# Two graph layers on one core: the prologue's vectors, transposes, weight loads and the order of the second pair's steps are rearranged

## The chip, the cores and the metric

The kernel runs on one core of one Trainium2 chip. A core has a matrix engine (TensorE, PE), three engines for elementwise work (VectorE or DVE, ScalarE or ACT, GpSimd or POOL), a queue engine (SyncE, SP) and 16 DMA engines. The metric is the device time of one execution in microseconds (us); the number of a kernel is the median of its runs.

## The reference

Inputs are x, 128 graphs of 128 nodes with 512 features, and adj, 128 matrices of 128 × 128 zeros and ones. All is fp32. Cut to what matters:

```python
# layer 0: graph attention, 8 heads of 64 units, then residual and layernorm
feats = einsum('bnf,hfu->bhnu', x, W)
e     = leaky_relu(e_self[..., :, None] + e_neigh[..., None, :], 0.2)
att   = softmax(e - 1e10 * (1 - adj))
x     = layernorm(x + relu(att @ feats + b0))
# layer 1: hypergraph convolution, twice, then residual and layernorm
H  = adj != 0;  w = adj[:, 0, :]
Dn = 1 / (H @ w);  Be = 1 / H.sum(axis=1)
conv(x, W, b) = Dn * (H @ (Be * (H.T @ (x @ W.T)))) + b
h  = layer_norm(relu(conv(x, W1, b1)), gamma, beta)      # 512 -> 1024
x  = layernorm(x + conv(h, W2, b2) + x)                   # 1024 -> 512
```

(The last line shows both residuals: the one inside the layer and the one around it.)

## The kernel before

The work is cut into 64 pairs of graphs; nodes lie in the 128 partitions. A pair passes through a software pipeline of some four periods of planned length T = 38.6. Its steps, in the names of the code:

- **Nodes and edges.** load (a: the two adjacency matrices; w: their first rows, to all partitions), load_edges (ab: adj in blocks of 32, in packets of 128 bytes), nodes (L334: D as a row, on DVE, seven instructions), write_nodes and spread_nodes (D through DRAM to all partitions, dnb), edges (L388: adj transposed in blocks of 32 by DVE from ab; H and its sums, be), scale_edges (hB = hT·be, L407), propagator (L411: pd = hB·hT on PE), r_evict (R = pd·dnb).
- **Features and attention.** x is transposed by DVE from blocks, for pairs 0 and 1 by PE (x_transpose_first, x_transpose_out). Features (pf) come from W0 with the attention vectors as two more columns. spread_rows and neighbours bring e_neigh through DRAM (rows, rd, nb) to all partitions. masked (L563, POOL) adds the mask, leaky (L579, ACT; for pair 0's last quarter two DVE instructions, L572 and L575), largest (L585, DVE), exponential (L593, ACT). The result is transposed (eT) by DVE from DRAM, for pair 0 by PE (e_transpose_first, pet). attend (pav) multiplies with the features, attended divides, add_bias (POOL), residual and moments, rstds (rsa, POOL), first_shift (sh), first_output.
- **Layer 1.** propagate (pz, L740), z_evict, z_sums; the products of W1 (ph, L775), h_sum, relu, squares; the products of W2 (py, L460); y_sum (L857), y_scale, the second propagation (pq), output. skip (L728) makes o = 2y + b2.

pf, ph and py are chains of seven block products (Strassen-Winograd): each has its own number in brackets here, as pyX(1) or pfW(3), and its products accumulate in banks X, Y and W of PSUM. Copies of X by ACT (L325) and sums by DVE join them. The weights need sums of their blocks for that: prepare_first_sums (W0), prepare_hidden (L228, W1: four sums s1 to s4), prepare_output_block_sums (L286, W2: four sums, by second_sums, L207).

**Weights and vectors.** W1 and W2 come in four blocks each by load_weights, all on ACT's queue. gamma, beta and b1 come by load_vectors (L170) with the partition as the fastest index, so each element is a packet of its own. gamma enters W2: prepare_output multiplies gamma and beta with W2 (pv, L257), prepare_output_sums copies (sums, ACT), prepare_output_spread (gw, bw, L269) spreads the two rows to 128 partitions by PE, prepare_output_blocks (L276) computes W2·gamma − gw in sixteen DVE instructions of 128 × 256.

**What sets the order.** No scheduler does. Every step has a lag and a time; all are put in one list, todo, and sorted by time, and instructions are issued in that order with each engine taking its own in sequence. For the first pairs a table, first, replaces the times by others, so the prologue's order is written out by hand. An engine that waits holds everything behind it in its own queue. A DMA that waits for its data or for a free buffer holds the queue of the engine that issues it.

The lists of the last 40 lines of the code (todo, first, and the loop that follows) are what the change edits most. As an example, this is how the weights' part of it stands:

```python
        (12.1, load_weights, (nc.scalar, w2_blocks, w2t, DH // 2, QU)),
        (13.45, load_vectors, (0,)), (14.05, load_weights, (nc.scalar, w1_blocks, w1t, F // 2, HALF)),
        (15.2, load, (1,)), (15.46, load_edges, (1,)), (16.1, load_vectors, (1,)),
        (79.1, prepare_hidden, (nc.gpsimd, 0)), (79.2, prepare_hidden, (nc.gpsimd, 1)),
```

Of the kernel before, what the change touches and what calls it, by code (L numbers as in the profile page):

```python
# [8 lines left out]
F32 = mybir.dt.float32  # L9
AF = mybir.ActivationFunctionType  # L10
ALU = mybir.AluOpType
# [9 lines left out]
def kernel(  # L21
# [73 lines left out]
    def load(p):  # L95
        s = st[p]
        gs = slice(2 * p, 2 * p + 2)
        s["a"] = work.tile([P, 2, N], F32, tag="a", name=f"a_{p}", bufs=2)
        nc.sync.dma_start(s["a"], adj[gs].rearrange("g n e -> n g e"))
        s["w"] = work.tile([P, 2, N], F32, tag="w", name=f"w_{p}")  # L100
        for g in range(2):
            nc.sync.dma_start(s["w"][:, g, :], adj[2 * p + g, 0, :].partition_broadcast(P))

# [54 lines left out]
    b1_sb = const.tile([P, KH], F32, name="b1_sb")  # L158
    gb = const.tile([P, 2, KH], F32, name="gb")
# [8 lines left out]
    load_edges(0)  # L168

    def load_vectors(some):  # L170
        queue = nc.sync
        if some == 0:
            for t, ap in ((gb[:, 0, :], gamma), (gb[:, 1, :], beta)):
                queue.dma_start(t, ap.rearrange("(k p) -> p k", p=P))
            everywhere(b0_bc, b0, queue)
        else:
            queue.dma_start(b1_sb, b1.rearrange("(k p) -> p k", p=P))
            everywhere(b2_bc, b2, queue)
# [204 lines left out]
    def x_transpose_out(p, s):  # L383
        s["xT"] = work.tile([P, 2, KF, N], F32, tag="xT", name=f"xT_{p}")
        for g in range(2):
            nc.scalar.copy(s["xT"][:, g].rearrange("p k n -> p (k n)"), s["px"][g])

    @step(1, 3.4)  # L388
    def edges(p, s):

        deg = small.tile([P, 2], F32, tag="deg", name=f"deg_{p}")
        hT = work.tile([P, 2, N], F32, tag="hT", name=f"hT_{p}")
        nc.vector.transpose(hT.rearrange("p g (b n) -> p (g b) n", b=NB), s["ab"])
        for g in range(2):
            nc.vector.tensor_scalar(
                hT[:, g, :], hT[:, g, :], 0.0, None, op0=ALU.not_equal, op1=ALU.add,
                accum_out=deg[:, g:g + 1],
            )
# [104 lines left out]
    def plain_features_out(p, s):  # L503
        s["ft"] = fts[p]
        for j in range(2):
            for g in range(2):
                (nc.scalar.copy, nc.vector.tensor_copy)[g](
                    s["ft"][:, g, j * HH:(j + 1) * HH, :UW], by_head(s["pf"][g][j])
                )
# [494 lines left out]
    for t, fn, *args in (  # L1004
# [47 lines left out]
        ("nodes", 2): 130.0, ("write_nodes", 2): 130.1, ("nodes", 3): 150.0,  # L1052
        ("write_nodes", 3): 150.1, ("skip", 0): 128.5,
# [5 lines left out]
    for p, time, fn, *args in (  # L1059
        (0, 11.4, x_transpose_first), (0, 11.5, x_transpose_out),  # L1060
        (0, 12.5, plain_features, 0), (1, 12.55, x_transpose_first),
        (0, 12.6, plain_features, 1), (0, 13.0, plain_features_out),
        (1, 13.8, x_transpose_out), (1, 14.5, plain_features, 0), (1, 14.6, plain_features, 1),
        (1, 15.6, plain_features_out),
# [77 lines left out]
```

## Time and profile before

| what | value |
|---|---|
| median of three runs | 2559.63 us (2559.15 to 2562.24) |
| profiled execution: its time | 2559.59 us |
| its span (first to last instruction) | 2557.8 us |
| instructions | 48296 |
| PE busy from 0 to 120 us | 93.8 us, the sum of the twelve rows of the table by stretch |
| PE busy from 120 to 159 us | 39.0 us |
| granted TensorE clock, whole run | 0.992 |

The profile is of one execution. "Busy" is the time in which an engine runs instructions; the granted clock is the share of its full clock that TensorE got, on average over a stretch. A line of a table by stretch has the stretch in us, its length, then for each of PE, the weight loads of PE (PEld), DVE, ACT and POOL the busy time and in brackets the number of instructions, then the clock, the share of the DMA engines that was busy, and GB/s. A line of waits has the engine, the line that waited, what released it, then the sum of the waiting time in us, the number and the longest. A line of a group has the line of the code, the engine, the operation, out<-in, the shapes, the number, then the busy time in us and the mean in ns, and behind the bar the idle time before it. An answer on one line of the code has the shortest, median and longest duration in ns, then the first and the last start in us.

### The profile page before, as it was taken

Reading aid. Unit: us, or ns where it says so; the run is one execution under the profiler, and the core shown is the slowest. Engines: PE = TensorE matmul, PEld = TensorE weight load, DVE = VectorE, ACT = ScalarE, POOL = GpSimd, SP = SyncE. Lnnn points to the kernel's source line nnn. Section 1 sums busy time; section 2 is a strip of 40 time slices with the busy share of each in tenths; the row PEclk is TensorE's granted clock in tenths of the full one; section 3 lists DMA queues with packets and bytes.
Section 4 is the critical chain, followed back from the end, with each engine's and each line's share of the span. In section 5 each row is a group of like instructions: output and inputs, shape, how many; then the busy total and the mean of one; then the engine's idle time right before and its main releaser. Section 6 shows DMA issues by size and latency. Waiting matters only on the chain.

```text
span 2557.8 us, 48296 instructions
## 1 busy us (share of the span) xinstructions
PE 2519.4 (98%) x16344; PEld 2281.6 (89%) x16344; DVE 2128.8 (83%) x4648; ACT 1514.0 (59%) x4291; POOL 1724.4 (67%) x1805
## 2 busy tenths in 40 slices
PE   7899999999999999999999999999999999999998
PEld 5799999999989999999999899989989998998997
DVE  5888888888888888888888888888888888888875
ACT  3556556557556566566565565565565665665653
POOL 4676766766766776766766666667667667666664
PEclk8999999999999999999999999999999999999999
DMA  6344454444444444444444544444444444444431
GB/s 180 100 141 137 131 145 133 134 143 133 133 140 140 136 137 138 142 133 141 141 134 128 148 138 128 145 130 134 143 139 135 134 141 142 133 127 147 138 111 50
DMA packets 426086, 343.99 MB, mean 134 GB/s; under 512 B 146544, under 2 KB 375408, under 8 KB 425840
## 3 DMA queue, kind: packets, MB, share of 16 engines
q1 hardware_dynamic: 421824, 335.40, 44.5%
q10 hardware_dynamic: 4016, 5.51, 0.7%
q8 instruction: 130, 2.13, 0.3%
q14 instruction: 116, 0.95, 0.1%
HBM read 239.09 MB, written 101.71 MB: 133 GB/s over the span
## 4 chain that ended last, share of the span: by engine, by line
PE 91%; DMA 4%; DVE 2%; issue 1%; POOL 1%; ACT 1%; SPq 0%; ACTq 0%; POOLq 0%; DVEq 0%
PE phX L775 18%; PE pyX L460 14%; PE pfX L460 9%; PE phW L775 9%; PE pav L649 8%; PE pyW L460 8%; PE pz L740 5%; PE phY L775 4%; PE pfW L460 4%; PE pq L898 4%; PE pyY L460 4%; PE pfY L460 2%; DMA nb<-rd 1%; PE pd L416 1%; DMA dnb<-dd_d 1%
## 5 line engine op out<-in xcount | busy, mean ns | idle before, releaser
L563 POOL TENSOR_TENSOR nb<-nb,neg 128x512 f32<-128x512 f32 x256 | 322.1, 1280 | 111.5 <-DMA nb<-rd 63.1
L775 PEld LDWEIGHTS phX<-zS,w_sb 128*128 128x128 f32 x3072 | 363.2, 192 | 32.5 <-issue 31.4
L325 ACT COPY py<-pyX 128x257 f32<-128x257 f32 x189 | 70.6, 374 | 539.3 <-PE pyX L460 535.7
L775 PE MATMUL phX<-zS,w_sb 128*128 128x128 f32 x3072 | 374.5, 276 | 1.8 <-POOL xS L442 1.0
L826 POOL TENSOR_TENSOR sq<-sq 128x512 f32<-128x512 f32 (+2 forms) x384 | 342.5, 892 | 24.0 <-ACT sq L815 2.2
L579 ACT ACTIVATE nb<-nb,ft 128x128 f32<-128x128 f32 x1020 | 323.7, 389 | 19.3 <-POOL nb L563 18.2
L593 ACT ACTIVATE nb<-nb,nm 128x128 f32<-128x128 f32 x1024 | 320.2, 392 | 3.9 <-DVE nm L585 3.8
L696 POOL TENSOR_TENSOR rso<-veo,mhalf 128x2 f32<-128x2 f32 x63 | 44.1, 700 | 333.4 <-DVE veo L694 317.8
L649 PEld LDWEIGHTS pav<-ft,eT 128*128 128x128 f32 x2048 | 253.4, 195 | 7.7
L680 DVE SCALAR_TENSOR_TENSOR y<-y,x 128x512 f32<-128x512 f32 x128 | 153.6, 1200 | 125.1 <-POOL y L673 125.1
L805 ACT ACTIVATE h<-h,b_sb 128x128 f32<-128x128 f32 x768 | 241.0, 392 | 17.1 <-DVE h L790 17.1
L649 PE MATMUL pav<-ft,eT 128*128 128x65 f32 x2048 | 247.3, 275 | 0.0
L460 PE MATMUL pyW<-w_sb,hS 128*128 128x256 f32 x1008 | 240.2, 380 | 6.5 <-DVE y L857 5.4
L460 PE MATMUL pyX<-w_sb,hS 128*128 128x257 f32 x1008 | 242.7, 383 | 0.6 <-ACT py L325 0.6
L460 PE MATMUL pyX<-w_sb,h 128*128 128x257 f32 x1008 | 240.0, 380 | 0.0
L460 PEld LDWEIGHTS pyW<-w_sb,hS 128*128 128x128 f32 x1008 | 189.6, 190 | 39.1 <-DVE y L857 11.5
L673 POOL TENSOR_TENSOR y<-y,b_bc 128x512 f32<-128x512 f32 x128 | 162.5, 1270 | 75.6 <-DVE y L664 75.6
L460 PEld LDWEIGHTS pyX<-w_sb,h 128*128 128x128 f32 x1008 | 187.4, 191 | 24.6
L460 PEld LDWEIGHTS pyX<-w_sb,hS 128*128 128x128 f32 x1008 | 186.5, 190 | 24.8 <-POOL y L673 0.9
L585 DVE TENSOR_REDUCE nm<-nb 128x4 f32<-128x512 f32 x256 | 173.6, 679 | 1.9 <-POOL zS L763 1.3
L442 POOL TENSOR_TENSOR xS<-xT 128x256 f32<-128x256 f32 x124 | 117.7, 949 | 80.6 <-DVE xT L366 80.6
L325 ACT COPY ph<-phX 128x512 f32<-128x512 f32 x192 | 112.3, 585 | 94.5 <-PE phX L775 91.3
(159 smaller groups left out, 5872.5 us busy)
## 6 DMA issues: line engine op xcount, KB each, us to landing
nb<-rd SPq DMA_DIRECT2D x127, 512.0 KB, 6.5
ed<-nb SPq DMA_DIRECT2D x126, 512.0 KB, 3.2
eb<-ed SPq DMA_DIRECT2D x504, 128.0 KB, 2.9
x<-in_x_dram SPq DMA_DIRECT2D x64, 512.0 KB, 7.3
out_dram<-o SPq DMA_DIRECT2D x63, 512.0 KB, 2.9
xb<-in_x_dram SPq DMA_DIRECT2D x248, 128.0 KB, 2.9
a<-in_adj_dram SPq DMA_DIRECT2D x64, 128.0 KB, 6.3
w<-in_adj_dram SPq DMA_DIRECT2D x128, 64.0 KB, 3.9
```

Of the source, the lines that this page charges most:

```text
L325: nc.scalar.copy(t[:, :n], s[kind, "X"][:, :n])
L460: nc.tensor.matmul(to[:, :n], lhs[:, k, :], rhs[:, k, :n], start=bool(start) and k == 0, stop=(k == nk - 1), skip_group_check=True,)
L563: nc.gpsimd.tensor_tensor(t, t, neg[:, :, None, :].to_broadcast([P, NB, HH, B]), op=ALU.add)
L579: nc.scalar.activation(t, t, AF.Prelu, bias=s["ft"][:, g, h, 0:1], alpha=SLOPE)
L585: nc.vector.tensor_reduce(s["nm"][:, g, hs], scores(p, s, g, hs).rearrange("p b h j -> p h b j"), AX.XY, ALU.max, negate=True,)
L593: nc.scalar.activation(t, t, AF.Exp, bias=s["nm"][:, g, h:h + 1])
L649: nc.tensor.matmul(t[:, h * (U + 1):(h + 1) * (U + 1)], s["eT"][:, g, q * HH + h, :], s["ft"][:, g, q * HH + h, 2:], start=True, stop=True,)
L673: nc.gpsimd.tensor_tensor(s["y"][:, g, :], s["y"][:, g, :], b0_bc, op=ALU.add)
L680: nc.vector.scalar_tensor_tensor(y, y, 0.0, s["x"][:, g, :], op0=ALU.max, op1=ALU.add)
L775: nc.tensor.matmul(to[:, m * N:(m + 1) * N], w[:, k, m * P:(m + 1) * P], rhs[:, k, :], start=bool(start) and m == 0 and k == 0, stop=(k == ...
L805: nc.scalar.activation(dst[:, k, :], src[:, k, :], AF.Relu, bias=b1_sb[:, c:c + 1])
L826: nc.gpsimd.tensor_tensor(t[:, :n, :], t[:, :n, :], t[:, n:2 * n, :], op=ALU.add)
```

## The change

It touches the prologue alone, which is the time before pairs follow each other in the steady order.

- gamma, beta and b1 are loaded as rows, 8 × 128 each, into one tile of 24 partitions (vec_rows); one PE transpose and one ACT copy make the columns (vecs). The loads stand early on SP's queue.
- adj of pairs 0 and 1 is transposed by PE (adj_transpose_first, bank pt) instead of by DVE from ab; the ab loads of these two pairs go.
- W1's blocks: the first two are issued by ACT, the other two by SP, the last first.
- Both copies of pair 1's features per half are on DVE.
- Three of the four hidden sums are on POOL (2, 0, 1, in this order), one on DVE; before it was two and two.
- The copies of sums are on DVE, not on ACT; gw and bw come ahead of attend(0,0,0) on PE; the first eight of the sixteen blocks of W2·gamma come between the two graphs' attended(0), the other eight in two groups of four.
- nodes(1) on DVE goes from before pair 0's scores to behind them, ahead of the first copies of eT. edges(1) goes behind sh of pair 0, pd_1 behind pz_0 on PE, R_1 behind h's first sum.
- skip(0) goes behind the h sums of pair 0, the two W2 sums on DVE are split and go further back, nodes(2) goes behind the first part of attended(1) of pair 1, ahead of the last feature sum (and of rows_2). The load of adj for pair 2 goes from 16.3 to 79.5, for pair 3 from 131 to 141.

The diff, cut to its core:

```diff
-    def load(p):
+    def load_adj(p):
         s = st[p]
-        gs = slice(2 * p, 2 * p + 2)
         s["a"] = work.tile([P, 2, N], F32, tag="a", name=f"a_{p}", bufs=2)
-        nc.sync.dma_start(s["a"], adj[gs].rearrange("g n e -> n g e"))
+        nc.sync.dma_start(s["a"], adj[2 * p:2 * p + 2].rearrange("g n e -> n g e"))
+    def load_first_row(p):
...
-    load_edges(0)
-    def load_vectors(some):
...
+    vec_rows = work.tile([3 * KH, P], F32, tag="neg", name="vec_rows", bufs=2)
+    for i, ap in enumerate((gamma, beta, b1)):
+        nc.sync.dma_start(vec_rows[i * KH:(i + 1) * KH], ap.rearrange("(k p) -> k p", p=P))
+    everywhere(b0_bc, b0, nc.sync)
+    load_adj(1)
...
+    def prepare_vectors():
+        t = bank("vecs_T")
+        nc.tensor.transpose(t[:, :3 * KH], vec_rows, ident[:3 * KH, :3 * KH])
+        nc.scalar.copy(vecs.rearrange("p v k -> p (v k)"), t[:, :3 * KH])
...
-            nc.scalar.copy(made["sums"][:, j * QU:(j + 1) * QU], made["pv"][j][:2, :QU])
+            nc.vector.tensor_copy(made["sums"][:, j * QU:(j + 1) * QU], made["pv"][j][:2, :QU])
...
+    def adj_transpose_first(p, s):
+        s["pt"] = bank(f"pt_{p}")
         for g in range(2):
+            nc.tensor.transpose(s["pt"][:, g * N:(g + 1) * N], s["a"][:, g, :], ident)
...
-        nc.vector.transpose(hT.rearrange("p g (b n) -> p (g b) n", b=NB), s["ab"])
+        if p < 2:
+            src = s["pt"][:, :2 * N].rearrange("p (g n) -> p g n", g=2)
+        else:
+            src = hT
+            nc.vector.transpose(hT.rearrange("p g (b n) -> p (g b) n", b=NB), s["ab"])
...
-                (nc.scalar.copy, nc.vector.tensor_copy)[g](
+                (nc.vector.tensor_copy if g or p else nc.scalar.copy)(
...
-        (13.45, load_vectors, (0,)), (14.05, load_weights, (nc.scalar, w1_blocks, w1t, F // 2, HALF)),
-        (15.2, load, (1,)), (15.46, load_edges, (1,)), (16.1, load_vectors, (1,)),
-        (79.1, prepare_hidden, (nc.gpsimd, 0)), (79.2, prepare_hidden, (nc.gpsimd, 1)),
+        (13.05, prepare_vectors, ()),
+        (14.05, load_weights, (nc.scalar, w1_blocks[:2], w1t, F // 2, HALF)),
+        (15.2, load_first_row, (1,)),
+        (15.46, load_weights, (nc.sync, w1_blocks[:1:-1], w1t, F // 2, HALF)),
+        (16.1, everywhere, (b2_bc, b2, nc.sync)),
+        (79.0, prepare_hidden, (nc.gpsimd, 2)), (79.1, prepare_hidden, (nc.gpsimd, 0)),
+        (79.2, prepare_hidden, (nc.gpsimd, 1)), (110.6, prepare_hidden, (nc.vector, 3)),
...
-        (79.0, prepare_rows, ()), (79.4, prepare_output_sums, ()),
-        (98.0, prepare_output_spread, ()), (98.1, prepare_output_bias, ()),
-        (110.6, prepare_hidden, (nc.vector, 2)), (110.7, prepare_hidden, (nc.vector, 3)),
-        (117.8, prepare_output_blocks, (slice(0, 1),)),
-        (118.1, prepare_output_blocks, (slice(1, 2),)),
-        (123.3, prepare_output_blocks, (slice(2, 4),)),
+        (78.3, prepare_rows, ()), (78.86, prepare_output_sums, ()),
+        (78.92, prepare_output_spread, ()), (79.35, prepare_output_bias, ()),
+        (99.75, prepare_output_blocks, (slice(0, 2),)),
+        (117.8, prepare_output_blocks, (slice(2, 3),)),
+        (118.1, prepare_output_blocks, (slice(3, 4),)),
         (126.5, prepare_output_block_sums, (nc.gpsimd, slice(0, 2))),
-        (132.0, prepare_output_block_sums, (nc.vector, slice(2, 4))),
+        (134.5, prepare_output_block_sums, (nc.vector, slice(2, 3))),
+        (137.5, prepare_output_block_sums, (nc.vector, slice(3, 4))),
...
-        ("r_evict", 0): 99.65,
-        ("spread_rows", 1): 15.72, ("nodes", 1): 15.8, ("write_nodes", 1): 15.85,
-        ("edges", 1): 15.9, ("scale_edges", 1): 15.95, ("neighbours", 1): 80.1,
-        ("propagator", 1): 98.2, ("spread_nodes", 1): 80.3, ("r_evict", 1): 110.9,
-        ("leaky", 0, 1, 1): 77.0,
+        ("r_evict", 0): 99.76,
+        ("spread_rows", 1): 15.72, ("nodes", 1): 78.67, ("write_nodes", 1): 78.68,
+        ("edges", 1): 110.4, ("scale_edges", 1): 110.5, ("neighbours", 1): 80.1,
+        ("propagator", 1): 117.76, ("spread_nodes", 1): 80.3, ("r_evict", 1): 121.8,
+        ("leaky", 0, 1, 1): 77.65,
...
-        ("attended", 0): 99.7,
+        ("attended", 0, 0): 99.7, ("attended", 0, 1): 99.8,
...
-        ("nodes", 2): 130.0, ("write_nodes", 2): 130.1, ("nodes", 3): 150.0,
-        ("write_nodes", 3): 150.1, ("skip", 0): 128.5,
+        ("nodes", 2): 139.5, ("write_nodes", 2): 139.6, ("nodes", 3): 150.0,
+        ("write_nodes", 3): 150.1, ("skip", 0): 132.5,
...
-            todo.append(({2: 16.3, 3: 131.0}.get(p, p * T), load, (p,)))
+            todo.append(({2: 79.5, 3: 141.0}.get(p, p * T), load, (p,)))
```

More of the change, by code (lines that the diff above doesn't have):

```diff
@@ L93 @@
     st = [{} for _ in range(PAIRS)]
-    def load(p):
+    def load_adj(p):
         s = st[p]
-        gs = slice(2 * p, 2 * p + 2)
         s["a"] = work.tile([P, 2, N], F32, tag="a", name=f"a_{p}", bufs=2)
-        nc.sync.dma_start(s["a"], adj[gs].rearrange("g n e -> n g e"))
+        nc.sync.dma_start(s["a"], adj[2 * p:2 * p + 2].rearrange("g n e -> n g e"))
+    def load_first_row(p):
+        s = st[p]
         s["w"] = work.tile([P, 2, N], F32, tag="w", name=f"w_{p}")
@@ L102, in load @@
             nc.sync.dma_start(s["w"][:, g, :], adj[2 * p + g, 0, :].partition_broadcast(P))
+    def load(p):
+        load_adj(p)
+        load_first_row(p)
     def load_rows(p, s):
@@ L156 @@
     )
-    b1_sb = const.tile([P, KH], F32, name="b1_sb")
-    gb = const.tile([P, 2, KH], F32, name="gb")
+    vecs = const.tile([P, 3, KH], F32, name="vecs")
+    gb, b1_sb = vecs[:, :2], vecs[:, 2]
     everywhere(an_bc, a_neigh, nc.scalar)
@@ L167 @@
     load(0)
-    load_edges(0)
-    def load_vectors(some):
[L171 to L178, printed above, removed]
+    vec_rows = work.tile([3 * KH, P], F32, tag="neg", name="vec_rows", bufs=2)
[3 more added lines that the diff above has]
+    load_adj(1)
     w2_sb = const.tile([P, 7, KH // 2, QU + 1], F32, name="w2_sb")
@@ L381, in x_transpose_first, with x_transpose_out @@
                 )
-    def x_transpose_out(p, s):
-        s["xT"] = work.tile([P, 2, KF, N], F32, tag="xT", name=f"xT_{p}")
+    def x_transpose_out(p, s, g):
+        if g == 0:
+            s["xT"] = work.tile([P, 2, KF, N], F32, tag="xT", name=f"xT_{p}")
+        nc.scalar.copy(s["xT"][:, g].rearrange("p k n -> p (k n)"), s["px"][g])
+    def adj_transpose_first(p, s):
+        s["pt"] = bank(f"pt_{p}")
         for g in range(2):
-            nc.scalar.copy(s["xT"][:, g].rearrange("p k n -> p (k n)"), s["px"][g])
+            nc.tensor.transpose(s["pt"][:, g * N:(g + 1) * N], s["a"][:, g, :], ident)
     @step(1, 3.4)
@@ L392, in edges @@
         hT = work.tile([P, 2, N], F32, tag="hT", name=f"hT_{p}")
-        nc.vector.transpose(hT.rearrange("p g (b n) -> p (g b) n", b=NB), s["ab"])
+        if p < 2:
[3 more added lines that the diff above has]
+            nc.vector.transpose(hT.rearrange("p g (b n) -> p (g b) n", b=NB), s["ab"])
         for g in range(2):
             nc.vector.tensor_scalar(
-                hT[:, g, :], hT[:, g, :], 0.0, None, op0=ALU.not_equal, op1=ALU.add,
+                hT[:, g, :], src[:, g, :], 0.0, None, op0=ALU.not_equal, op1=ALU.add,
                 accum_out=deg[:, g:g + 1],
@@ L1059 @@
     for p, time, fn, *args in (
-        (0, 11.4, x_transpose_first), (0, 11.5, x_transpose_out),
+        (0, 11.4, x_transpose_first), (0, 11.5, x_transpose_out, 0), (0, 11.5, x_transpose_out, 1),
         (0, 12.5, plain_features, 0), (1, 12.55, x_transpose_first),
-        (0, 12.6, plain_features, 1), (0, 13.0, plain_features_out),
-        (1, 13.8, x_transpose_out), (1, 14.5, plain_features, 0), (1, 14.6, plain_features, 1),
-        (1, 15.6, plain_features_out),
+        (0, 12.6, plain_features, 1), (0, 12.65, adj_transpose_first),
+        (0, 13.0, plain_features_out), (1, 13.1, x_transpose_out, 0), (1, 13.8, x_transpose_out, 1),
+        (1, 14.5, plain_features, 0), (1, 14.6, plain_features, 1),
+        (1, 15.6, plain_features_out), (1, 97.9, adj_transpose_first),
         (0, 78.8, e_transpose_first, 0, 0), (0, 78.85, e_transpose_first, 0, 1),
```

## The prediction

> **What bounds the kernel now.** I read the page's busy shares and chain of work first, then a table of busy time by stretch, then the waits of TensorE (PE) and ScalarE (ACT), then groups and single instructions of VectorE (DVE) and GpSimd (POOL) in the prologue. The page says that nothing but TensorE can be late for most of the run:
>
> ```profile
> PE 2519.4 (98%) x16344; PEld 2281.6 (89%) x16344; DVE 2128.8 (83%) x4648; ACT 1514.0 (59%) x4291; POOL 1724.4 (67%) x1805
> PE 91%; DMA 4%; DVE 2%; issue 1%; POOL 1%; ACT 1%; SPq 0%; ACTq 0%; POOLq 0%; DVEq 0%
> ```
>
> The table by stretch (length, busy PE, weight loads, DVE, ACT, POOL, then granted clock) shows where the other 38 us lie:
>
> ```profile
> 40.00:50.00 10.00, 7.19 (x30) 5.80 (x31) 8.20 (x15) 4.90 (x16) 2.91 (x5) 0.61 0.74 112
> 50.00:60.00 10.00, 8.92 (x28) 5.96 (x26) 5.82 (x14) 1.69 (x4) 4.50 (x4) 0.50 0.57 131
> 60.00:70.00 10.00, 8.07 (x50) 7.91 (x51) 8.69 (x15) 7.01 (x19) 9.29 (x9) 0.70 0.01 2
> 70.00:80.00 10.00, 7.88 (x66) 7.37 (x66) 9.90 (x24) 7.99 (x26) 6.04 (x6) 1.00 0.46 157
> 80.00:90.00 10.00, 5.63 (x32) 4.45 (x31) 9.84 (x16) 4.98 (x17) 4.81 (x5) 1.00 0.31 76
> 90.00:100.00 10.00, 9.83 (x31) 8.44 (x32) 3.40 (x10) 1.84 (x5) 8.32 (x8) 0.50 0.23 60
> 120.00:159.00 39.00, 39.00 (x256) 35.20 (x255) 32.24 (x72) 23.56 (x68) 26.90 (x29) 1.00 0.45 136
> ```
>
> From 120 us on PE never idles (39.00 of 39.00). So the change can only move the moment at which that steady train starts. I take as its mark pz_1, the propagate product of pair 1, at 115.71 us; everything behind it is shifted rigidly. Before the mark there are idle PE and half clock: 42.1 to 66.0 us and 89.9 to 100.15 us at 0.5. Three waits carry it:
>
> ```profile
> PE pfX L460 <- ACT pf L325: 4.5, 1, 4.5
> PE pyW L460 <- DVE y L857: 1.3, 1, 1.3
> ACT ft L507 <- DMA w<-in_adj_dram: 12.5, 1, 12.5
> ```
>
> The first: PE stands from 85.66 to 90.17 because a copy by ACT stands behind relu of h(1,0), which stands behind DVE, which does skip(0), nodes(2) and two weight sums first (79.65 to 87.86). The half clock after it covers 10.24 us of work that would need 5.1. The third: ACT hangs at the issue of the last two W1 loads until 34.4.
>
> **What the Trainium skill says.** "SBUF — State Buffer", section "SBUF: two separate sides": DVE and POOL share a port pair as a lock held for a whole instruction; a DVE operation with two SBUF inputs blocks against POOL. The trace agrees. Beside POOL's two sums (the last line, here from a view of that line) one of the two L407 took 2111 ns, the other 281, and L572 1658 against the 692 of L575, which has the same shape and ran free:
>
> ```profile
> L407 DVE TENSOR_SCALAR hB<-hT,deg 128x128 f32<-128x128 f32 x2 | 2.3, 1194 | 0.0
> L572 DVE TENSOR_TENSOR nb<-nb,ft 128x512 f32<-128x512 f32 x1 | 1.7, 1658 | 0.0
> L575 DVE SCALAR_TENSOR_TENSOR nb<-nb 128x512 f32<-128x512 f32 x1 | 0.7, 692 | 0.0
> L234 POOL TENSOR_TENSOR w_sb<-w_sb x1: 2417/2417/2417, 40.5 to 40.5; 128x1024 f32<-128x1024 f32 x1
> ```
>
> "TensorE: Matmul & The Clock Gate", Part 1: after idle time of about one window of 3.4 us PE gets half its clock. The trace agrees: 0.5 after the idle stretches 37.94–41.79 and 85.66–90.17. Part 4 adds that transposes don't count as busy in the same way, which fits the half clock that stays through 46–59. "DMA: Bandwidth & Descriptors", section "Issuing engines are not separate DMA queues": a second queue saves issue time only. That fits the third wait above, which is issue time.
>
> **The change, part by part.**
>
> *Vectors as rows.* Three loads of 1024 elements, two of which landed at 16.2 and 19.3, become three short ones and a transpose. First use is the pv products at 30.86, so 11 us cover either. Added: one transpose (0.14, as px at 12) and one small copy (about 0.2) beside pf_0. If the cover were gone, pv would wait one for one. Value 0, ends −0.3 and +0.5.
>
> *adj by TensorE.* Out: eight block loads and two stream transposes on DVE (0.446 each). In: four PE transposes of 0.14. Those of pair 0 lie in the 2.4 us in which PE waits for xT (18.99 to 21.41), those of pair 1 ahead of pz_0, where PE waits for y. Value 0 on the path, ends −0.4 and +0.3.
>
> *W1 over two queues, copies of ft_1 to DVE.* ACT is free at about 25 in place of 34.4. leaky then follows the masks: three groups of four, 29.98 to 33.7 (12 × 0.30); the exponentials come next and end about 40 with the fourth, 47.2 before. By itself that brings the first products of attention 6 us earlier. DMA bytes are the same.
>
> *Three hidden sums on POOL at once.* POOL held two at 38.04 and 40.46. Now it runs three from 34.3 (masks and sel end 34.29, the W1 blocks landing by 33.6) to about 41.7 and longer with the lock (2.34 each). On DVE the leaky pair and nodes(1) stand in the same stretch: leaky's second step, two node products and the small ones each let POOL through or wait for it. Free they would end at 37.6. Alternating with 2.34 each I get 34.3 + 2.34 (sum) + 0.69 (leaky) + 2.34 + 0.28 + 2.34 + 0.28 + 1.2 (rest, nodes(1) is 1.3 in all) = 43.8. I take 43.8; the ends are 37.6 and 43.8. In exchange DVE loses one L234 (2.30 or 1.21) at 60–64.
>
> *eT copies, sums, gw/bw.* They stand behind nodes(1) on DVE: two copies at 0.60 and two for sums at about 0.35 end at 45.7. Then the two products for gw and bw, now ahead of attention on PE and cold: pitch 1.87 + 1.84 = 3.71. Attention starts at 49.4, where it started at 46.39. Gone is the same 3.7 that lay at 54.0 to 57.7 behind attention and cost nothing, since PE waited for y then. From y to pz_0 the steps are as before: pz_0 from 61.27 to **about 64.7 (+3.4)**. pd_1 now stands between pz_0 and ph: +1.1 cold.
>
> *ph to pf.* The ph chain had 0.66 + 1.0 + 0.99 of idle time from ACT's copies and h, which take up part of it: its end goes from 81.67 to 84.4 (+2.7).
>
> *Skip, nodes(2), weight sums behind h(1,0).* h(1,0) comes 0.7 after ph's end, at 85.1 (before 87.78). The 4.5 us of idle PE and the half clock go: from 81.67 to pyX(1) at 99.0 were 17.3; less 4.5 and 5.1 that is 7.7; so pyX(1) at 92.1, 6.9 earlier. If TensorE alone set the end, pz_1 would come at 92.1 + (115.71 − 99.0 − 1.3) = 107.5: **8.2 earlier**.
>
> *What is late next.* DVE gets in that stretch what it was spared before: skip 1.4, transposes 0.9 + 0.4, sum L211 1.5, ft 0.4, transposes 1.3, L211 1.5, y of pav_1 1.2, nodes(2) 1.3, ft 0.4; then rows_2. Free that ends at 96.4 from 85.1, with every lock (add_bias 1.27, squares and hS of POOL 1.27 each) at 100.4; I take 98.4. Before it was 99.77 to 100.01, right behind PE. And rows_2 starts the longest chain of this stretch: rd_2 written at 100.04 to 101.47, nb_2 read until 106.51, mask on POOL 106.67, rsa behind it on POOL's queue 108.04, sh 108.79 (1.22 by the lock), largest 110.14, nodes(3) 110.74 to 113.5 (its products 0.64 and 1.35, by the lock), then y L857 113.81, pyW at 113.87. That chain is 13.8 long, its order in the queues is the same after the change, and +0.3 for the adj of pair 3 loaded in SP's queue ahead of nb_2. So y is at 98.4 + 13.8 + 0.3 = 112.5. PE, ready for it at 107.5 − 1.9 = 105.6, stands 6.9 us and gets half the clock: 3.4 to 6.8 us of it, a loss of 1.7 to 3.4. pz_1, or what it stands for: 112.5 + 1.9 + 1.7…3.4 = 116.1 to 117.8, against 115.71.
>
> **Sum.** +0.4 to +2.1, middle +1.2, on the profiled execution's 2559.59 (span 2557.8 and 1.8 around it), which is the median of 2559.63 within 0.04: **2560.8 us**. The expected gain is turned into a new wait.
>
> **Rivals.**
> (1) *TensorE sets the end all the same.* DVE comes to rows_2 with PE, near 92.4; y at 106.5, no half clock: pz_1 at 108.3, 7.4 earlier, 2552.2. For it: 4.5 us of idle PE and 5.1 of half clock are plainly in the table, and 3.40 of 10 busy on DVE from 90 to 100 means spare time there. Against: the queue on DVE from 85.1 to rows_2 adds up to 11.3 without any lock. Half of the locks and an early phase without them (nodes(1) at 37.6, all 2.7 earlier) give 2557 to 2559, which is the likeliest case's lower part.
> (2) *The lock decides, and it is slower.* Place: POOL's three sums against nodes(1), and POOL's squares, hS and add_bias against skip, L211 and nodes(2). rows_2 at 101; y at 115.1; PE idle 9.5 us; half clock as long as the 10.24 after 85.66, which costs 5.1: pz_1 at 115.1 + 1.9 + 5.1 = 122.1, 6.4 later, **2566.0**. It decides from rows_2 at 99.7 with 5.1 of clock loss, at 101.4 with 3.4. For it: every lock counted did occur in before, 2.11, 1.66, 2.30 and 1.35 long. Against: DVE often got in between.
> (3) *The loads were hidden anyway and nothing moves.* ACT's 12.5 us end in exponentials that nodes(1) then replaces as the last; it ends within 2559 to 2561, on the forecast's side, and is counted there.
>
> **Chances.** About 0.2%, 5.1 us, is what a measurement of this kernel can tell from no change, so faster is below 2554.5 and slower above 2564.7. Forecast with (3), 2555.5 to 2564.5: 0.46. Rival 1, 2551 to 2554.5: 0.27. Rival 2, 2564.7 to 2568: 0.27. Bounds of the small parts are within these. The range for 8 in 10 leaves the outer ends of both: 2551.8 to 2566.6.
>
> **What would show it.** Right: the 12.5 us on ft and the 4.5 us on pf gone from the waits; nodes(1) with products of over 1 us at 35 to 44; attention at about 49; h(1,0) at 85; rows_2 at 98; a wait of PE for y L857 of 5 to 8 us in place of 1.3; pz_1 at 116 to 118. Wrong: attention before 46 (no lock on nodes(1), then all is 3 to 6 us earlier); rows_2 directly behind PE at 92 to 94 (rival 1); or any PE idle time behind 120, since I take the steady train as unmoved.

## The result, and the profile after

The changed kernel takes 2558.88 us (median of 6 runs, 2557.01 to 2560.6), the kernel before on the same occasions 2558.56 us (6 runs, 2556.34 to 2562.24). The ratio is 1.000, 95% interval 0.9987 to 1.0012: no difference. The prediction of 2560.8 us was right in its number, and the new wait that it named is in the trace. The number was right in part by luck: two parts that I had put at nothing are worth 4 to 5 us, and the other parts cost about 3 us more than I had reckoned.

The page of the changed kernel: PE is busy 7.4 us less, but the span of this execution is only 1.2 us shorter (2557.8 before).

```profile
span 2556.6 us, 48295 instructions
PE 2512.0 (98%) x16349; PEld 2275.0 (89%) x16349; DVE 2134.2 (83%) x4649; ACT 1513.1 (59%) x4288; POOL 1726.3 (68%) x1806
```

The table by stretch of the changed kernel, with the columns as before:

```profile
40.00:50.00 10.00, 6.70 (x18) 4.19 (x19) 4.25 (x11) 0.00 (x0) 0.67 (x4) 0.60 0.11 28
50.00:60.00 10.00, 5.24 (x26) 4.84 (x25) 8.31 (x22) 1.07 (x2) 3.34 (x3) 0.50 0.52 129
60.00:70.00 10.00, 7.58 (x52) 7.50 (x52) 8.70 (x19) 5.97 (x16) 7.45 (x10) 0.71 0.02 4
...
80.00:90.00 10.00, 10.00 (x63) 9.09 (x62) 8.00 (x11) 6.31 (x18) 7.84 (x6) 1.00 0.55 122
90.00:100.00 10.00, 9.55 (x52) 8.23 (x52) 9.38 (x22) 1.12 (x3) 7.90 (x8) 1.00 0.08 19
100.00:110.00 10.00, 3.56 (x20) 2.86 (x18) 5.30 (x10) 3.36 (x9) 6.48 (x6) 0.84 0.82 195
110.00:120.00 10.00, 8.28 (x43) 7.54 (x44) 7.62 (x26) 4.43 (x15) 2.57 (x5) 0.65 0.25 30
120.00:159.00 39.00, 39.00 (x260) 35.59 (x259) 32.02 (x71) 23.92 (x68) 26.73 (x30) 1.00 0.45 136
```

From 80 to 100 the idle PE and the half clock are gone: 19.55 of 20 busy at full clock, where the kernel before had 15.46 at 0.75. The same table shows where that went: 100 to 110 has PE busy for 3.56 (10.00 before), and the clock is 0.65 in the next ten. The waits of PE in the first 130 us of the changed kernel name it (line numbers differ between the kernels: L474, L754, L789 and L871 here are L460, L740, L775 and L857 before):

```profile
PE pyW L474 <- DVE y L871: 8.2, 1, 8.2
PE pz L754 <- ACT y L731: 7.2, 1, 7.2
PE gw L274 <- DVE sums L269: 6.6, 1, 6.6
```

The 4.5 us wait for the feature copy is no longer in the list, nor ACT's 12.5 us in ACT's own; the wait for y (1.3 us before) is now 8.2. The timeline of the changed kernel shows what stands ahead of that y on DVE:

```profile
104.70 1.26 POOL L577 TENSOR_TENSOR nb<-nb,neg 128x512 f32<-128x512 f32 x1 [3.52 <-DMA nb<-rd]
105.92 0.71 POOL L710 TENSOR_TENSOR rsa<-vea,mhalf 128x2 f32<-128x2 f32 x1
106.67 1.22 DVE L725 SCALAR_TENSOR_TENSOR sh<-mva,rsa 128x2 f32<-128x2 f32 x1 [3.42 <-POOL rsa L710]
107.80 0.67 DVE L599 TENSOR_REDUCE nm<-nb 128x4 f32<-128x512 f32 x1
...
109.17 1.34 DVE L346 SCALAR_TENSOR_TENSOR w<-a,w 128x128 f32<-128x128 f32 x1
...
111.29 0.38 DVE L871 TENSOR_TENSOR y<-py,pyW 128x256 f32<-128x256 f32 x1
...
111.72 3.78 PE L474 MATMUL pyW<-w_sb,hS 128*128 128x256 f32 x8 [8.16 <-DVE y L871]
```

y needs none of them (e1 below issues it ahead of them). DVE waits 3.42 us for rsa, which waits on POOL behind a mask, which waits for a DMA. PE then runs pyW at half clock: 3.78 us for what took 2.00 in the kernel before:

```profile
113.87 2.00 PE L460 MATMUL pyW<-w_sb,hS 128*128 128x256 f32 x8 [1.28 <-DVE y L857]
```

pz_1 starts at 115.30 (115.71 before) and the ph products of pair 1 at 117.92 (117.49 before): the steady train starts where it did.

### The profile page after: what moved, and what is told of

Same layout as the page of the kernel before. It is cut to its first block, busy times and chain, and to the rows that moved or that the text cites. A ratio compares the mean times of both kernels' runs of the same rounds, so it can differ in the third digit from the quotient of the medians.

```text
span 2556.6 us, 48295 instructions
## 1 busy us (share of the span) xinstructions
PE 2512.0 (98%) x16349; PEld 2275.0 (89%) x16349; DVE 2134.2 (83%) x4649; ACT 1513.1 (59%) x4288; POOL 1726.3 (68%) x1806
## 4 chain that ended last, share of the span: by engine, by line
PE 91%; DMA 3%; DVE 3%; issue 1%; POOL 1%; ACT 0%; SPq 0%; POOLq 0%; DVEq 0%
PE phX L789 18%; PE pyX L474 15%; PE phW L789 9%; PE pfX L474 9%; PE pyW L474 8%; PE pav L663 8%; PE pz L754 5%; PE phY L789 4%; PE pq L912 4%; PE pfW L474 4%; PE pyY L474 4%; PE pfY L474 2%; DMA nb<-rd 2%; PE pd L430 1%; DMA rd<-rows 1%
## 5 line engine op out<-in xcount | busy, mean ns | idle before, releaser
L789 PEld LDWEIGHTS phX<-zS,w_sb 128*128 128x128 f32 x3072 | 363.1, 192 | 33.0 <-issue 31.5
L789 PE MATMUL phX<-zS,w_sb 128*128 128x128 f32 x3072 | 374.4, 275 | 2.2 <-POOL xS L456 1.3
L593 ACT ACTIVATE nb<-nb,ft 128x128 f32<-128x128 f32 x1020 | 323.9, 389 | 30.6 <-POOL nb L577 27.8
L474 PE MATMUL pyW<-w_sb,hS 128*128 128x256 f32 x1008 | 241.9, 382 | 12.3 <-DVE y L871 11.0
L819 ACT ACTIVATE h<-h,vecs 128x128 f32<-128x128 f32 x768 | 240.8, 392 | 11.6 <-DVE h L804 11.6
L474 PE MATMUL pyX<-w_sb,hS 128*128 128x257 f32 x1008 | 242.7, 382 | 1.0 <-ACT py L330 1.0
L474 PE MATMUL pyX<-w_sb,h 128*128 128x257 f32 x1008 | 239.4, 379 | 0.0
L474 PEld LDWEIGHTS pyW<-w_sb,hS 128*128 128x128 f32 x1008 | 190.3, 190 | 45.0 <-DVE y L871 16.8
L474 PEld LDWEIGHTS pyX<-w_sb,hS 128*128 128x128 f32 x1008 | 186.0, 190 | 25.9 <-POOL y L687 0.9
L474 PEld LDWEIGHTS pyX<-w_sb,h 128*128 128x128 f32 x1008 | 186.4, 190 | 24.7
```

The lines of the kernel that those rows point to most:

```text
L474: nc.tensor.matmul(to[:, :n], lhs[:, k, :], rhs[:, k, :n], start=bool(start) and k == 0, stop=(k == nk - 1), skip_group_check=True,)
L593: nc.scalar.activation(t, t, AF.Prelu, bias=s["ft"][:, g, h, 0:1], alpha=SLOPE)
L789: nc.tensor.matmul(to[:, m * N:(m + 1) * N], w[:, k, m * P:(m + 1) * P], rhs[:, k, :], start=bool(start) and m == 0 and k == 0, stop=(k == ...
L819: nc.scalar.activation(dst[:, k, :], src[:, k, :], AF.Relu, bias=b1_sb[:, c:c + 1])
```

## Experiments

Each run was timed in five rounds against the kernel before on the same chip; the ratio is to that. Besides, I give the start of pz_2, the propagate product of pair 2, counted from rows_0 (the first scores leaving DVE), since that start alone lies between 19.5 and 21.7 us in the traces, as x lands earlier or later. pz_2 from rows_0 is 135.0 before and 135.4 after, and it lies behind all of the prologue. The mark shows, in one execution, where time was won; whether it was kept is for the ratio to say. From pz_2 to the end the profiled executions took 2401.2 to 2403.4 us, in e12 2406.1. The changed kernel is itself known only to 0.13% against the kernel before (about 3 us), so small ratios of its variants are read together with the mark.

| run | what | ratio to before, 95% | pz_1 | pz_2 |
|---|---|---|---|---|
| before | | | 96.2 | 135.0 |
| after | | 1.000 (0.9987–1.0012) | 95.9 | 135.4 |
| e1_ysum_first | after, y first | 0.9987 (0.9979–0.9995) | 89.4 | 132.2 |
| e2_chain_off | e1, pair 1's rsa and output first | 0.9983 (0.9977–0.9990) | 86.2 | 131.0 |
| e3_nodes2_back | after, nodes(2) behind rows_2 | 0.9998 (0.9990–1.0006) | 94.0 | 132.9 |
| e4_before_ysum_first | before, y first | 0.9995 (0.9987–1.0003) | 92.7 | 132.0 |
| e5_zT_ahead | e2, zT first | 0.9987 (0.9979–0.9995) | 86.1 | 132.2 |
| e6_hidden_on_dve | after, hidden sums on DVE | 0.9977 (0.9968–0.9986) | 90.7 | 129.6 |
| e7_both | e5 and e6 | 0.9961 (0.9948–0.9973) | 79.0 | 123.9 |
| e8_w1_one_queue | after, W1 on one queue | 1.0008 (1.0000–1.0016) | 96.8 | 135.8 |
| e9_pair2_behind | e7, nodes(3), two masks and a leaky later | 0.9953 (0.9939–0.9967) | 79.0 | 123.6 |
| e10_loads_as_before | after, vectors and adj loaded as before | 1.0016 (1.0009–1.0022) | 100.2 | 139.0 |
| e11_gw_behind | after, gw/bw and eight W2 blocks behind attention | 0.9993 (0.9986–0.9999) | 92.9 | 132.7 |
| e12_loads_alone | before, vectors and adj loaded as after | 0.9979 (0.9972–0.9986) | 90.1 | 128.8 |

**Does the order on DVE hold the end?** My theory: the 8.2 us wait for y is the order alone. The rival: pair 2's scores are as late as that anyway, and what PE wins it gives back. e1 adds two due times to the changed kernel:

```diff
+        ("y_sum", 0, 1, 1, 2, "W"): 148.92, ("first_shift", 1): 148.95,
```

> The changed kernel with one sum of pair 0's output, y L871 (graph 1, half 1), issued on VectorE ahead of sh, the largest value and nodes(3), which it needs nothing of. Theory (the order on VectorE makes TensorE wait): y at 103.5 to 104 in place of 111.67, the 8.2 us wait of pyW shrinks to under 1, the next wait is pz_1 for pair 1's normalised y, which comes at about 108.7 by the mask and sh that stand ahead of it; the steady train starts 5 to 7 us earlier, 2552 to 2554. Rival (pair 2's scores are late anyway, since rows_2 and nb_2 don't move): TensorE runs ahead and waits later, at the attention of pair 2; no gain, 2558 to 2559.

e2 has these and three more:

```diff
+        ("masked", 2, 0, 0): 147.4, ("first_output", 1, 0): 148.96, ("first_output", 1, 1): 148.97,
```

> As the run before, and besides: rsa of pair 1 goes ahead of pair 2's first mask on GpSimd, and pair 1's normalised output ahead of pair 2's first leaky on ScalarE, so pair 1 no longer waits for pair 2's DMA. Theory: pz_1 at about 105.5, no half clock, steady train 8 to 10 us earlier, 2549 to 2551. Rival: nothing gained, or less than in the run before, because pair 2's scores come later still; TensorE waits after 120 us.

Waits of PE from 100 to 160 us in e1:

```profile
PE pz L754 <- ACT y L731: 3.1, 1, 3.1
PE phX L789 <- ACT zT L766: 1.3, 1, 1.3
```

The wait for y is gone in both, and pz_1 is 6.5 and 9.7 us earlier, as the theory had it. But pz_2 is only 3.1 and 4.4 us earlier, and the times are 0.13 and 0.17% below the kernel before (3.3 and 4.4 us): about half of what each was to bring. Theory and rival were both half right. In e2 PE waits 3.2 us for zT (ACT's copies of pz_1), which stands behind pair 2's leaky on ACT, and the clock is halved behind that. So e5 moves that too:

```diff
+        ("leaky", 2, 0, 1): 156.41, ("leaky", 2, 1, 0): 156.42,
+        ("largest", 2, 0, 1): 156.5, ("largest", 2, 1, 0): 156.55,
```

> As the second run (y sum, rsa and normalised output of pair 1 ahead of pair 2's scores), and besides the copies of pair 1's zT ahead of eight of pair 2's leaky instructions on ScalarE. Theory (each step of pair 1 stood behind steps of pair 2 that wait for DMA, on three engines one after the other): the 3.2 us wait of phX for zT and the half clock behind it (113 to 118 us) go, pz_2 comes at 147.5 to 149 in place of 152.5, the time is 4 to 5 us below that of the second run, about 9 us below the kernel before. Rival (pair 2's scores take it back): pz_2 as in the second run, with a new wait of TensorE for zS or for eT of pair 2.

The theory fell here, the rival held. The wait for zT is 0.6 us, and in its place there is one for zS, the sums of zT on POOL (waits of PE in e5):

```profile
PE phX L789 <- POOL zS L777: 3.4, 1, 3.4
```

zS stands behind rsh (POOL's step for the layernorm of h), and what rsh needs stands behind nodes(3) and R_2 on DVE; pz_2 is 1.2 us later than in e2. With the next stall as long as the last, each of these fixes is worth little by itself.

e3 tests the other end of the chain, with nodes(2) behind rows_2:

```diff
-        ("nodes", 2): 139.5, ("write_nodes", 2): 139.6, ("nodes", 3): 150.0,
+        ("nodes", 2): 141.0, ("write_nodes", 2): 141.1, ("nodes", 3): 150.0,
```

> The changed kernel with nodes(2) behind rows_2 on VectorE, in place of ahead of it. Theory: rows_2 at 93 to 94 in place of 97.0, the whole chain behind it 3 to 4 us earlier, y L871 at 108, 3 to 5 us less in all: 2554 to 2556. Rival (the last wait is from the early part of the prologue, the locks of the three hidden sums and gw/bw ahead of attention): rows_2 earlier, but no gain, 2558 to 2559.

rows_2 came at 73.3 in place of 77.6 from rows_0, and nb_2 was still issued at 78.3 (80.0 after): SP's queue has the rows of pair 3 and the write of nodes(2) ahead of it, and these wait for nodes(2). Only 1.8 us were left at pz_1, and the time is not distinguishable from before. I had followed rows_2 to nb_2 through the landing of rd alone and not through SP's queue.

e4 makes e1's edit in the kernel before (its line is e1's):

```diff
+        ("y_sum", 0, 1, 1, 2, "W"): 148.92, ("first_shift", 1): 148.95,
```

> The kernel before with the same sum y L857 issued ahead of sh, the largest value and nodes(3). Theory: TensorE waited 1.28 us for it there, so at most 1.3 to 2 us are to be had: 2556.5 to 2558. Rival (this order costs the same in both kernels): 5 to 7 us less, as in the changed kernel.

PE's 1.28 us wait for y is gone there, the ratio is 0.9995 with 1 inside its interval: no more than the wait was to be had, as the theory had it. pz_2 from rows_0 moved by more, 3.1 us, but 1.6 of that lies ahead of pz_0 (41.7 from rows_0 before, 40.1 in e4), where the edit changes nothing; from pz_0 to pz_2 it is 1.5, close to the wait. In these two executions the start of attention did not follow rows_0, so a mark counted from rows_0 is uncertain by some 1.6 us against the kernel before.

**What does the early part cost?** e6 takes the three hidden sums from POOL and puts all four on DVE where DVE waited for attention:

```diff
-        (79.0, prepare_hidden, (nc.gpsimd, 2)), (79.1, prepare_hidden, (nc.gpsimd, 0)),
-        (79.2, prepare_hidden, (nc.gpsimd, 1)), (110.6, prepare_hidden, (nc.vector, 3)),
+        (78.93, prepare_hidden, (nc.vector, 2)), (78.94, prepare_hidden, (nc.vector, 0)),
+        (78.95, prepare_hidden, (nc.vector, 1)), (78.96, prepare_hidden, (nc.vector, 3)),
```

> The changed kernel with all four hidden sums on VectorE in the 5 us in which it waits for attention, none on GpSimd. Theory: nodes(1) loses its three stalls by the lock (5.9 us) and ends at about 35.5; the products for gw start at 38 to 39 in place of 43.3, attention at 42 to 43 in place of 47.0, pz_0 at 58 in place of 62.4. As the chain behind rows_2 starts where the products of W1 end, all of it is passed on: pz_1 4 us earlier, 2554 to 2555. Rival (the end is set by something that doesn't move with attention, such as nb_1's loads or pair 1's exponentials on ScalarE): attention earlier, pz_1 within 1 us of 115.3.

DVE's groups from 34 to 44 us, first in the changed kernel, then in e6 (L346 and L351 are nodes(1)):

```profile
L346 DVE SCALAR_TENSOR_TENSOR w<-a,w 128x128 f32<-128x128 f32 x2 | 4.1, 2080 | 0.0
L351 DVE TENSOR_SCALAR dn<-dd 128x2 f32<-128x2 f32 x1 | 2.4, 2357 | 0.0
```

```profile
L346 DVE SCALAR_TENSOR_TENSOR w<-a,w 128x128 f32<-128x128 f32 x2 | 0.5, 282 | 0.0
L351 DVE TENSOR_SCALAR dn<-dd 128x2 f32<-128x2 f32 x1 | 0.2, 170 | 0.0
```

Three instructions lose 5.8 us to POOL's sums, and one of them writes 2 numbers to a partition. Without that, attention starts at 43.1 (47.0) and pz_0 at 58.6 (62.4), both 5.2 us earlier if counted from rows_0, and all of it is passed on: pz_2 5.8 us earlier, 0.23% below the kernel before. The theory was right. The wait of 8.1 us for y is still there; it moved along with the rest.

e11 puts gw and bw behind attention again, and with them the eight W2 blocks that need gw:

```diff
-        (78.92, prepare_output_spread, ()), (79.35, prepare_output_bias, ()),
-        (99.75, prepare_output_blocks, (slice(0, 2),)),
+        (98.0, prepare_output_spread, ()), (98.1, prepare_output_bias, ()),
+        (110.7, prepare_output_blocks, (slice(0, 2),)),
```

> The changed kernel with the products for gw and bw behind the first attention products on TensorE again, and the eight W2 instructions that need gw behind the last hidden sum on VectorE. Theory (the two products cost 3.7 us on the path since nothing hides them there): attention at 43.3 in place of 47.0, pz_0 3.5 us earlier, passed on to rows_2 as far as the ph stage lets it: 2 to 3.7 us less in all. Rival (the eight instructions, 3.1 us, delay VectorE in the ph stage instead): pz_0 earlier, but h and rows_2 at their old place, the same time.

The wait of PE is now at pav (5.4 us, for eT). pz_0 comes 3.4 us earlier, 59.0, or 5.3 if counted from rows_0, so up to pz_0 the two products were on the path in full, and part of the eight blocks (3.3 us of DVE) with them. Then phX waits 2.8 us for ACT and runs at half clock behind that. At pz_2 2.7 us are left, in the time 0.07% (1.8 us): between theory and rival.

e7 has the edits of e5 and e6 together, cut here to two of their lines:

```diff
+        (78.95, prepare_hidden, (nc.vector, 1)), (78.96, prepare_hidden, (nc.vector, 3)),
...
+        ("leaky", 2, 0, 1): 156.41, ("leaky", 2, 1, 0): 156.42,
```

> Both edits of this call. Theory: their gains add, pz_2 at 144 to 145, 13 us below the kernel before, 2546 to 2548. Rival: no more than the better one of the two alone.

They add, and more: 0.39% (10 us) below the kernel before, pz_2 11.4 us below the changed kernel, where e6 alone had 5.8 and e5 3.2. The forecast of 13 us was somewhat too much; PE still waits 3.5 us for zS. e9 goes after that wait:

```diff
-        ("nodes", 2): 139.5, ("write_nodes", 2): 139.6, ("nodes", 3): 150.0,
-        ("write_nodes", 3): 150.1, ("skip", 0): 132.5,
+        ("nodes", 2): 139.5, ("write_nodes", 2): 139.6, ("nodes", 3): 153.5,
+        ("write_nodes", 3): 153.6, ("skip", 0): 132.5,
...
+        ("leaky", 2, 0, 1): 156.41, ("leaky", 2, 1, 0): 159.5,
+        ("largest", 2, 0, 1): 156.5, ("largest", 2, 1, 0): 159.6,
+        ("masked", 2, 1, 0): 159.3, ("masked", 2, 1, 1): 159.4,
```

> As the run with both edits (hidden sums on VectorE, pair 1's output steps and zT ahead of pair 2's scores), and besides nodes(3) behind the variance of h on VectorE and two of pair 2's masks behind zS on GpSimd. Theory: the 3.5 us wait of phX for zS and the half clock behind it (110 to 114 us) go, pz_2 comes at 139 to 141 in place of 145.5, 4 to 6 us less than with both edits alone. Rival (now pair 2's scores are really late): a wait of 3 us or more at pav or ph of pair 2 in its place, pz_2 at 144 to 146, the same time as with both edits.

Its waits of PE from 40 to 160 us:

```profile
PE phX L789 <- ACT ph L330: 2.5, 2, 2.3
...
PE phX L789 <- POOL zS L777: 0.8, 1, 0.8
```

The wait for zS fell from 3.5 to 0.8, one for ph's copy on ACT took its place, with half clock behind it (3.63 us for a product of 1.95). pz_2 is within 0.3 us of e7. The rival was right that a wait would take its place, if not which. At 2546.18 us against 2558.84, ratio 0.9953, it has the lowest ratio of all; against e7 it is not told apart.

**The loads.** e8 gives all of W1 to ACT's queue again:

```diff
-        (14.05, load_weights, (nc.scalar, w1_blocks[:2], w1t, F // 2, HALF)),
+        (14.05, load_weights, (nc.scalar, w1_blocks, w1t, F // 2, HALF)),
...
-        (15.46, load_weights, (nc.sync, w1_blocks[:1:-1], w1t, F // 2, HALF)),
```

> The changed kernel with all four loads of W1 issued by ScalarE again, as in the kernel before. Theory: ScalarE hangs at the third and fourth issue until about 33, leaky and exponentials come 5 us later than in the changed kernel, attention at 49 to 51 in place of 47.0, pz_1 2 to 4 us later: 2561 to 2563. Rival (the loads were hidden, a queue more saves nothing on the path): attention at 47, same time.

The theory was wrong: ACT hung at the fourth issue alone, until 27.86, just behind the landing of nb at 27.84, and leaky waited for POOL's first mask until 29.05 in any case. Attention from rows_0 is 0.6 us later, pz_2 0.5, the time 0.08%, at the edge of its interval. So the second queue is not what freed ACT. e10 undoes the other parts, with the new order kept:

```diff
-        nc.sync.dma_start(vec_rows[i * KH:(i + 1) * KH], ap.rearrange("(k p) -> k p", p=P))
+        nc.sync.dma_start(vecs[:, i], ap.rearrange("(k p) -> p k", p=P))
...
+    load_edges(0)
     load_adj(1)
...
-        if p < 2:
+        if p < 0:
...
-        (13.05, prepare_vectors, ()),
...
-        (15.2, load_first_row, (1,)),
+        (15.2, load_first_row, (1,)), (15.3, load_edges, (1,)),
...
```

> The changed kernel with gamma, beta and b1 loaded as columns and adj of pairs 0 and 1 loaded in blocks and transposed by VectorE, as in the kernel before. Theory (both were forecast at nothing): pv within 1 us, attention within 1 us, time within 0.1% of the changed kernel. Rival (thousands of small packets delay x, adj and W1, all loads pass the same 16 engines): x_1, rd_1 and W1 land 1 to 3 us later, attention and the end 1 to 3 us later.

The rival was right, the forecast of nothing wrong: 0.16% slower than before (interval 0.09 to 0.22%); pz_2 3.6 us behind the changed kernel. The scores of pair 0 land 3.7 to 4.5 us after their issue (1.4 to 1.6 in the changed kernel, for the two that its trace tells) and nb lands 10.3 us after rows_0 (7.1). Of these 3.2 us, 0.9 is that the last of the scores was issued later, and 2.2 that they took longer to land. No W1 issue on ACT hung in this run, but the last two of W2 did, until 19.4 and 20.2, so W2 was under way when the scores left (at 21.5 to 22.8). Here the small loads stand in another place than in the kernel before, so this says what they cost in the new order. e12 asks the reverse, these parts alone in the old order. Its edit to the kernel before is the change's own for vec_rows, prepare_vectors, adj_transpose_first and edges and for the early load_adj(1) (as in the diff above), and in the list:

```diff
-        (13.45, load_vectors, (0,)), (14.05, load_weights, (nc.scalar, w1_blocks, w1t, F // 2, HALF)),
-        (15.2, load, (1,)), (15.46, load_edges, (1,)), (16.1, load_vectors, (1,)),
+        (13.05, prepare_vectors, ()), (14.05, load_weights, (nc.scalar, w1_blocks, w1t, F // 2, HALF)),
+        (15.2, load_first_row, (1,)), (16.1, everywhere, (b2_bc, b2, nc.sync)),
```

> The kernel before with this part of the change alone: gamma, beta and b1 as rows through one product, adj of pairs 0 and 1 early and transposed by TensorE; W1 stays on ScalarE's queue, all steps keep their old times. Theory (it is the number of transfers in flight, not the queue, that held ScalarE's issues back): the issues of the last two W1 blocks no longer hang until 34, leaky starts at about 30 in place of 34.9, nb lands 1 to 2 us earlier, attention at 43 to 45 in place of 46.4, and as the 4.5 us wait for the feature copy stays, 1.5 to 3.5 us less in all. Rival (nothing of it was on the path, as forecast): attention within 1 us of 46.4, the same time.

The theory was right, and its 1.5 to 3.5 us too little: 0.21% below the kernel before (5.4 us; interval 0.14 to 0.28%), leaky at 31.2 (34.9), attention at 42.1 (46.4). ACT's timeline, first of the kernel before, then of e12:

```profile
24.41 0.49 ACTq L127 DMA_DIRECT2D w<-in_w1t_dram  x1
30.60 3.74 ACTq L127 DMA_DIRECT2D w_sb<-in_w1t_dram  x2
34.38 0.66 ACT L507 COPY ft<-pf 128x264 f32<-128x264 f32 x2 [12.53 <-DMA w<-in_adj_dram]
```

```profile
23.74 0.49 ACTq L134 DMA_DIRECT2D w<-in_w1t_dram  x1
24.26 3.90 ACTq L134 DMA_DIRECT2D w_sb<-in_w1t_dram  x2
29.15 0.38 ACT L522 COPY ft<-pf 128x264 f32<-128x264 f32 x1 [6.45 <-DMA w<-in_adj_dram]
```

Issuing a load takes 0.4 to 0.5 us. What held the third and fourth W1 load back before were waits of 5.7 and 3.0 us: they were issued at 30.60 and 33.97, and the first W1 block landed at 30.58, a row of adj of pair 1 at 33.94. The trace has eight semaphores by which all these transfers report, and each late one had the semaphore of the one that had just landed. With fewer transfers in the list the third does not wait and the fourth waits only until 27.8. Packets in the first 60 us, before, after and in e12:

```profile
DMA packets 17587, 11.52 MB, mean 192 GB/s; under 512 B 8624, under 2 KB 15280, under 8 KB 17584
```

```profile
DMA packets 12172, 11.24 MB, mean 187 GB/s; under 512 B 3185, under 2 KB 9865, under 8 KB 12169
```

```profile
DMA packets 12339, 11.25 MB, mean 188 GB/s; under 512 B 3352, under 2 KB 10032, under 8 KB 12336
```

The scores of pair 0 leave at 19.7 to 20.3 us in both kernels. In the kernel before, gamma and beta have landed by then; what the scores meet are the blocks of W2. The packets from 12 to 20 us, before and after, then the busy share of the DMA engines from 20 to 24 us in 40 slices, before and after:

```profile
DMA packets 3940, 1.73 MB, mean 217 GB/s; under 512 B 2331, under 2 KB 3889, under 8 KB 3940
DMA packets 2445, 2.35 MB, mean 293 GB/s; under 512 B 88, under 2 KB 2383, under 8 KB 2445
DMA  9999999999999999988842000000000000000000
DMA  2000023000320000000000000007495597795996
```

W2's four loads are issued at nearly the same times (11.71 to 14.11, and 12.03 to 13.58), but with the small packets 0.6 MB less passes from 12 to 20 us, and the engines stay full until about 22 us. There the last block of W2 landed at 22.8, and the scores at 22.9 to 23.5. I read it as the small packets having delayed W2, and W2 the scores; no run shows that order of causes by itself.

## Why the prediction was right, and where it wasn't

The time was right, and so was the step that the prediction rested on most, *What is late next.* Forecast were rows_2 at 98.4, y at 112.5, PE idle for 6.9 us, half the clock, pz_1 at 116.1 to 117.8. Measured: rows_2 at 97.0, y ready at 111.67, idle 8.16, the clock halved, pz_1 at 115.30. e1 and e2 confirm that this wait was of order only, and that taking it away is worth 3 to 4 us and not the whole 8 to 10, since pair 1's other steps stand behind pair 2's too. One sum in this step is wrong: the list of what DVE does ahead of rows_2 adds up to 10.3 us, not to the 11.3 that I used. With 10.3, rows_2 comes out at 97.4 (97.0 measured) and the total about 1 us lower.

*Three hidden sums on POOL.* The mechanism was right and is shown by e6: nodes(1) ended at 41.3 (forecast 43.8, since POOL began at 32.9 and not at 34.3). I gave it 6.2 us over the free end; e6 recovers 5.8 at pz_2.

*eT copies, sums, gw/bw.* 3.71 was forecast for the two products, 3.68 lies between gw at 43.30 and attention at 46.98. Up to pz_0 it was on the path in full, as e11 shows; behind pz_0 about half of that was lost again: e11 gets 2.7 us at pz_2 and 1.8 in the time.

*pz_0 at +3.4, ph's end at +2.7.* Too late by 2.3 and 2.6: measured 62.42 (61.27) and 81.80 (81.67). (The +3.0 at attention became +3.4 at pz_0 without any working.) The next point more than accounts for it: e10, without those two parts, has pz_0 3.9 us later from rows_0 than the changed kernel.

*Vectors as rows* and *adj by TensorE*: these steps failed. "Value 0, ends −0.3 and +0.5" was reasoned from the first use of gamma, which does have cover. It left out what else the transfers hold up: the scores of pair 0 (3.1 to 3.3 us to landing before, 1.4 to 1.6 after), and ACT's issues, which wait for earlier landings. Measured in place of 0: 5.4 us in the old order (e12), about 4 in the new (e10).

*W1 over two queues.* Failed in the cause. I ascribed ACT's 12.5 us to issue time, and the end of it to the second queue, and agreed with the Trainium skill on it ("DMA: Bandwidth & Descriptors", "Issuing engines are not separate DMA queues"). That a second queue saves little is what e8 shows (0.08%). That the 12.5 us were issue time the page doesn't say, and the timeline of the kernel before refutes it: five issues took 2.0 us of them, the wait for the scores to land 1.7, and the waits for a semaphore 8.7.

*Skip, nodes(2), weight sums behind h(1,0).* Right: no wait of 4.5, no half clock, pyX(1) at 89.8 (forecast 92.1, before 99.0).

*The total.* That it came out right is in part luck. e10 is the changed kernel without the two parts that I had put at nothing. It is 0.16% (4.1 us) slower than the kernel before, where my sum for all the other parts was +1.2. So the other parts cost about 3 us more than I had reckoned, the two parts brought back the 4 us that I had left out, and the errors nearly cancel. From the side of the old order it is the same: e12 gains 5.4 us, and the rest of the change takes as much again. The single runs price the lock at 5.9 us (e6), the order at the end at 4.4 (e2) and gw with its blocks at 1.8 (e11), 12 in all. That the rest of the change brought the difference back, above all by taking the 4.5 us stall away, is inferred: no run took that edit out alone.

Rival 2's place was right, its price too high; rival 1 fails in that DVE's queue did not reach rows_2 with PE (pfW(3) began at 88.93, rows_2 at 97.00).

Not settled: how e12's 5.4 us divide between fewer packets, fewer waits for a semaphore and the earlier load of pair 1's adj (no run parted them), what each of vectors and adj brings alone, and what a version with e7's edits and gw behind attention would take.

## What to carry to other kernels

When a stall is removed ahead of a steady stage, follow each engine's queue, the DMA queues too, to the next step that waits for something unrelated; the gain ends there, and steps of the pair that is about to run should not stand behind steps of the next pair that wait for DMA. Two engines that share a lock should get their long and short operations in different stretches: 7.6 us of sums on one stretched three instructions of 0.2 to 0.3 us to 1.7 to 2.4 us on the other. A load with cover for its own use is not free: count the packets that pass ahead of the load that has none, and the issues that wait for it to land. A wait at an issue looks like issue time in a list of issues: compare it with the length of one issue and with the last landing before it.

## What the runs showed of the hardware

A VectorE instruction on 128 × 2 values, with one input, took 2357 ns beside a GpSimd sum and 170 ns without (L351 in the changed kernel and in e6). From the Trainium skill ("SBUF — State Buffer", "SBUF: two separate sides") I had quoted the condition for two SBUF inputs. It covers L572 and L346, but neither L351 nor the L407 that I showed beside L572, which read one tensor. The section names a mode of VectorE that uses two ports as another condition; that these two ran in it no run here shows.

A write of 4 KB of scores landed after 3.1 to 3.3 us in the kernel before, where the DMA engines were full with W2, and after 1.4 to 1.6 us in the changed kernel, where they were mostly idle. An issue of a DMA held its engine for 5.7 us while an earlier transfer with the same semaphore was under way.

Half clock followed idle times of PE of 2.3 us (e9) and 2.4 us (before, at 21.4) up to 8.2 us (after). The shortest are below the 3.4 us quoted in the prediction. Once PE was busy again it lasted from 2.9 us (e11, products of W1) to 10.0 us (before, from 90.17, features and attention). The half clock from 46 to 59 us, which I laid to transposes, is not explained by them: they are 1.65 of the 12.92 us in which PE was busy there.
